# Moving a block's transfers from GpSimd's queue to SyncE's in a LayerNorm, attention and ternary feed-forward kernel

## The chip, the core and the metric

The kernel runs on one core of a Trainium2 chip. A core has a matrix engine (TensorE, PE in the profile; its weight loads are PEld), a vector engine (VectorE, DVE), an activation engine (ScalarE, ACT), a general engine (GpSimd, POOL) and a sequencer without arithmetic (SyncE, SP). Each engine works through its own list of instructions in order; a DMA is an instruction on one of these lists, and while it waits for its turn or for a semaphore, everything behind it on that list waits too. The metric is the device time of one execution in microseconds.

## The reference

The input x is 2048 rows of 256 numbers, all float32. With xn the layer norm of x, the output is x plus an attention of 16 heads of 128 over xn, plus a gated feed-forward over xn whose weights are rounded to -1, 0 or 1:

```
qkv = einsum('bsd,ed->bse', xn, Wqkv)          # 3 x 16 heads of 128
logits = einsum('bqhd,bkhd->bhqk', q, k) * 128 ** -0.5
out = einsum('bhqk,bkhd->bqhd', softmax(logits), v)
y = x + einsum('bse,de->bsd', out, Wout) + ffn(xn)
ffn(xn) = (sigmoid(xn @ t(w1)) * (xn @ t(w2))) @ t(w3)
```

Here t(w) divides a weight by its mean magnitude, rounds, clips to -1..1 and transposes.

## The kernel before, in words

After a lead-in (norm, first head's q, k and v, the feed-forward), the kernel walks 64 *blocks*: a block is one head and 512 of the 2048 queries, four blocks to a head. A block has four *steps* of 128 queries (t = 0 to 3), and one pass of the main loop (line 965) is one step. The pass does work for two places at once: scores, exponentials and exchange for step v, and, six steps behind (`LEAD`), the product with the values for block n, step t (`divmod(u, TB)`).

In a pass `scores` puts 128 by 2048 logits in PSUM (PE), DVE takes their maxima, ACT takes exponentials into `p`. The product with v needs the exponentials transposed. `exchanged` (line 595) moves the off-diagonal quarters of `p` into `part` with twelve DMAs, ten issued from SP and two from ACT, and ACT copies the four diagonal quarters; `transposed` (line 652) lets DVE turn 32 by 32 pieces of `part` into `R`, two passes later. `part` has two buffers, so the exchange of step v waits until DVE has transposed step v - 2. GpSimd forms differences of `R` (line 677) for a fast product with seven instead of eight multiplications, `weighted` (line 706) is that product, and `copied` and `added` combine its quarters in `oU`.

The order on every engine is written out by hand (`manual_schedule`): an instruction stands on its engine's list where the loop calls it.

Around a block there are transfers that are no exchange:
- `inverses` (line 615) stores the reciprocals of the softmax sums to DRAM (`rd`), and `spread` (line 630) reads them back to all partitions into `oT`, by which `added` scales `oU`.
- `put_away` (line 777) stores `oU` to DRAM (`od`).
- The output projection is also a fast product. It is done two heads (a *group*) at a time, in blocks 0 to 3 of the next group: `o_fetched` (line 787) brings two heads' stored outputs back into the three slots of `o3`, `o_product` (line 803) multiplies them with the group's part of Wout, into the PSUM tile `pow`, and `o_read` (line 817) lets DVE add the result to the running sum of the output, `osums`. `osums` holds two of the four query quarters; `y_moved` (line 793) stores one to DRAM (`yd`) and brings the next one back. `o_moved` (line 826) and `between` (line 929) say in which block and step each of these is called.
- `load_weights` (line 73) loads the weights of the next group.

Most of them are called from `between`, at the end of a pass and so after that pass's exchange. The times at which the sum's data must be there follow from the two-step rhythm: of the fetches and returns in `o_moved`, `y_moved` at (block, step) (0, 0), (1, 3) and (2, 0) is read by `o_read` in the next pass, and `o_fetched` at (1, 0) and (3, 0) is read by `o_product` at the end of the next pass. The DMAs of the last blocks (lines 858, 867, 913 and 957) stand outside the change.

Of the kernel before, what the change touches and what calls it, by code (L numbers as in the profile page):

```python
# [20 lines left out]
def layernorm_attention_bitffn_kernel(  # L21
# [14 lines left out]
    nc = tc.nc  # L36
# [9 lines left out]
    TB = QB // P  # L46
# [4 lines left out]
    G = 2  # L51
# [21 lines left out]
    def load_weights(g: int, what: str, queue=nc.sync):  # L73

        if what == "o":
            w = wpool.tile([P, G, DM], F32, tag="wvo", name=f"wo{g}")
            src = woutT[g * G * D : (g + 1) * G * D, :].rearrange("(h p) e -> p h e", p=P)
        else:
            tag = "wvo" if what == "v" else f"w{what}"
            w = wpool.tile([P, KC, G * D], F32, tag=tag, name=f"w{what}{g}")  # L80
            lo = "qkv".index(what) * HD + g * G * D
            src = wqkvT[:, lo : lo + G * D].rearrange("(c p) e -> p c e", p=P)
        queue.dma_start(w, src)
        weights[g, what] = w
# [60 lines left out]
    def weight_sums(h: int):  # L145
        wk, wq = (weights[h // G, i][:, :, bass.ts(h % G, D)] for i in "kq")
        w = wpool.tile([P, 4, D], F32, tag="ws", name=f"ws{h}")
        add, sub = ALU.add, ALU.subtract
        nc.gpsimd.tensor_tensor(w[:, 0], wq[:, 0], wq[:, 1], add)
        nc.gpsimd.tensor_tensor(w[:, 1], w[:, 0], wk[:, 0], sub)  # L150
        nc.gpsimd.tensor_tensor(w[:, 2], wk[:, 0], wq[:, 0], sub)
        nc.gpsimd.tensor_tensor(w[:, 3], wk[:, 1], w[:, 1], sub)
        ws[h] = w
# [70 lines left out]
    o3 = const.tile([P, 3, QB], F32, tag="o3", name="o3")  # L224
# [57 lines left out]
    def v_read(g: int, m: int, second: bool, pm):  # L282
# [14 lines left out]
    ods = [  # L297
        [away.tile([P, G, QB], F32, tag=f"od{g}_{c}", name=f"od{g}_{c}") for c in range(NB)]
        for g in range(2)
    ]  # L300
    rds = [away.tile([P, 32], F32, tag=f"rd{i}", name=f"rd{i}") for i in range(2)]
# [313 lines left out]
    def inverses(n: int):  # L615
        if n >= NBK - NB:

            r = small.tile([P, TB], F32, tag="rlast", name=f"rlast{n}")
            nc.vector.tensor_tensor(r, sums[n][:, :, 0], sums[n][:, :, 1], ALU.add)
            nc.vector.reciprocal(r, r)  # L620
            rbs[n] = r
            return
        ri, riT = rinvs[n % 2]
        nc.vector.tensor_reduce(ri[:, :TB], sums[n], AX.X, ALU.add)
        nc.vector.reciprocal(ri[:, :TB], ri[:, :TB])

        nc.vector.transpose(riT, ri)  # L627
        nc.gpsimd.dma_start(rds[n % 2], riT)  # L628

    def spread(n: int):  # L630

        if n < NBK - NB:
            r = rds[n % 2].rearrange("(j c) r -> j (c r)", c=32)[:, : TB * 32]
            nc.gpsimd.dma_start(
                oT.rearrange("p (j x) -> p j x", j=P // 32), r.partition_broadcast(P)
            )
            rbs[n] = oT
# [3 lines left out]
    for n in range(1, len(blocks)):  # L641
        a, b, c, d, e = roles[-1]
# [142 lines left out]


    def o_fetched(g: int, b: int, head: int, slot: int):
        nc.gpsimd.dma_start(o3[:, slot], ods[g % 2][b][:, head])

    def o_difference(slot: int, x: int, y: int):  # L790
        nc.gpsimd.tensor_tensor(o3[:, slot], o3[:, x], o3[:, y], ALU.subtract)

    def y_moved(b: int, back: bool):
        y, yd = osums[:, 1 - b % 2], yds[b]
        nc.gpsimd.dma_start(*((yd, y) if back else (y, yd)))

    def o_sums(g: int):
        w = weights[g, "o"]
        sums_of(w[:, :, :P], w[:, :, P:], f"wos{g}")
# [26 lines left out]
    def o_moved(g: int, i: int, t: int):  # L826

        pair, a = divmod(i, 2)
        b, more = 2 * pair, pair == 0
        keep = g == H // G - 2 and pair  # L830
        if (a, t) == (0, 0):
            y_moved(b + 1, False)
        elif (a, t) == (0, 1):
            o_fetched(g, b, 1, 1)
        elif (a, t) == (0, 3):
            o_difference(2, 1, 2)
        elif (a, t) == (1, 0):
            o_fetched(g, b + 1, 1, 0)
        elif (a, t) == (1, 1):
            if not keep:  # L840
                y_moved(b, True)
            if more:
                o_fetched(g, b + 3, 1, 2)
        elif (a, t) == (1, 2):
            if more:
                o_fetched(g, b + 3, 0, 1)
                o_fetched(g, b + 2, 0, 0)
        elif (a, t) == (1, 3) and more:
            y_moved(b + 2, False)
            o_difference(1, 1, 0)  # L850
            o_difference(2, 2, 1)
# [4 lines left out]
    def fetched_back(b: int):  # L856

        nc.gpsimd.dma_start(xnT[:, :, bass.ts(b, QB)], yds[b])

    def x_fetched(b: int):  # L860
        if b % 2 == 0:
            tag, bufs = (("v", 3), ("kT", 2))[b // 2]
            y = kvpool.tile([P, S], F32, tag=tag, name=f"ya{b}", bufs=bufs)
            y = y.rearrange("p (b t d) -> p b t d", b=2, d=DM)
            sofar[b], sofar[b + 1] = y[:, 0], y[:, 1]
        nc.gpsimd.dma_start(
            sofar[b], x[b * QB : (b + 1) * QB, :].rearrange("(t p) d -> p t d", p=P)
        )
# [60 lines left out]
    def between(n: int, t: int):  # L929

        g, i = divmod(n, GB)
        last = NBK - NB

        if t == 1:
            if i == GB - 1 and n < last:
                load_weights(g, "o", nc.gpsimd)
        if t == 2:
            if i == NB - 1 and g + 1 < H // G:
                load_weights(g + 1, "v", nc.gpsimd)
            elif n == last - 1:  # L940
                load_weights(g, "o", nc.gpsimd)
        if g and i < NB:
            o_moved(g - 1, i, t)
        elif n < last:
            if i == GB - 2:
                if t < 3:
                    o_fetched(g, *((0, 0, 0), (1, 0, 1), (1, 1, 2))[t])
                else:
                    o_difference(1, 1, 0)
                    o_difference(2, 2, 1)  # L950
            elif (i, t) == (GB - 1, 2):
                y_moved(0, False)
        if n < last and (i, t) == (GB - 1, 3):
            o_sums(g)
        if n >= last - 1 and t == 2:
            b = n + 1 - last
            nc.gpsimd.dma_start(o3[:, b % 2], ods[(H - 2) // G % 2][b][:, 0])
        if (n, t) in ((last - 2, 3), (last - 1, 0)):
            fetched_back(n + 2 - last)
        if t == 0 and n in (last - 3, last - 2, last, last + 1):  # L960
            x_fetched((last - 3, last - 2, last, last + 1).index(n))

    behind = []
    with tc.manual_schedule():
        for u in range(-LEAD, (NBK - 1) * TB):
            n, t = divmod(u, TB)
            v = u + LEAD
            lead_in = u < 0
            more = v < NBK * TB
            h, b = blocks[v // TB] if more else (H, 0)  # L970
# [7 lines left out]
            g, i = divmod(n, GB)  # L978
# [22 lines left out]
            if t == 0 and n >= 0:  # L1001
                if 0 < n <= NBK - NB:
                    put_away(n - 1)
                differences(n, "T1b")
            elif t == 1 and n >= 0:
                differences(n, "T2h")
                if n >= NB and n % GB < NB and n % 2 == 0 and n < NBK - NB:
                    o_difference(0, 2, 0)
                differences(n, "T3b")
                spread(n)  # L1010
                if blocks[n][1] == 0:
                    v_combined(blocks[n][0], 2)
                    v_combined(blocks[n][0], 3)
                differences(n, "T4")
            elif t == 3 and -1 <= n < NBK - 2:
                differences(n + 1, "T1a")
                if n % 2 and n % GB < NB <= n < NBK - NB - 2:
                    y_moved(n % GB, True)
                differences(n + 1, "T3a")
                if n >= 0 and blocks[n + 1][1] == 0:  # L1020
                    v_combined(blocks[n + 1][0], 0)
                    v_combined(blocks[n + 1][0], 1)
# [23 lines left out]
                    q_piece(1, b)  # L1046
            if b == NB - 1 and h + 2 < H:
                if h % G == 0 and v % TB in (0, 1):
                    load_weights(h // G + 1, "qk"[v % TB], nc.gpsimd)
                if v % TB == 3:  # L1050
                    weight_sums(h + 2)
            twice = seven and twice
            if t == 2 and -1 <= n < NBK - 1:
                inverses(n + 1)
# [30 lines left out]
            if u >= 0:  # L1085
                if t == 0:
                    differences(n, "T2l")
                between(n, t)

        n = NBK - 1  # L1090
# [50 lines left out]
```

## Time and profile before

| | |
|---|---|
| median of 3 runs | 2158.83 us (2158.8 to 2162.86) |
| profiled execution, its own time | 2159.7 us |
| its span | 2157.9 us |
| PE busy | 2143.5 us |
| DVE, ACT, POOL busy | 1756.1, 1375.1, 1579.3 us |
| bytes moved by DMA | 304.34 MB, 141 GB/s in the mean |
| DMAs issued from SP in the main loop | 2560 exchanges, 64 KB each |

The profile gives, for one execution, the busy time of each engine, the DMAs with the median time from issue to landing, and groups of instructions by line. A wait is written as engine and line, what ended the wait, then the total in us, how often, and the longest. A row of the timeline has its start and its duration in us from the span's start, then engine, line, operation and tiles; "SPq" is SP's queue of DMAs, and what stands in square brackets is the idle time of the engine before the row and what ended it.

### The profile page before, as it was taken

What the parts mean: (1) busy time and instruction counts of PE and PEld (TensorE: products, weight loads), DVE (VectorE), ACT (ScalarE), POOL (GpSimd) and SP (SyncE); (2) the same over time, 40 slices, a digit from 0 to 9 for tenths busy, and PEclk for the clock granted to TensorE, in tenths of its full rate; (3) what the DMA queues carried; (4) which work ended last, traced back from release to release, by engine and by line L of the source; (5) the groups of instructions that cost most, each with busy time, mean ns of one, the idle gap of its engine ahead of it and who ended that gap; (6) DMA issues with size and microseconds to landing.
All of it is one profiled execution on the core that took longest, in us unless ns stands there. A gap on an engine that the chain in (4) does not pass through costs nothing. (4 is left out here: it accounts for less than half of the span.)

```text
span 2157.9 us, 41390 instructions
## 1 busy us (share of the span) xinstructions
PE 2143.5 (99%) x14018; PEld 1207.6 (56%) x14018; DVE 1756.1 (81%) x2394; ACT 1375.1 (64%) x2414; POOL 1579.3 (73%) x1010
## 2 busy tenths in 40 slices
PE   9999999999999999999999999999999999999999
PEld 6745445445655555555555455655555555555556
DVE  6577887888888887888788888788888888788885
ACT  5587766666666666666666666666666666666773
POOL 0067767987678867887768876788767887788873
PEclk9999999999999999999999999999999999999999
DMA  2055555575556655566555754556555665556663
GB/s 94 39 119 139 132 117 136 148 187 142 121 140 160 166 141 128 136 184 157 123 128 142 189 151 110 140 145 180 149 122 135 157 173 143 127 138 184 174 151 95
DMA packets 182341, 304.34 MB, mean 141 GB/s; under 512 B 55088, under 2 KB 60592, under 8 KB 182128
## 3 DMA queue, kind: packets, MB, share of 16 engines
q1 hardware_dynamic: 127856, 175.21, 31.9%
q0 software_dynamic: 28720, 91.97, 17.5%
q10 hardware_dynamic: 25552, 34.51, 6.2%
q8 instruction: 111, 1.82, 0.4%
q14 instruction: 102, 0.84, 0.1%
HBM read 65.60 MB, written 34.54 MB: 46 GB/s over the span
## 5 line engine op out<-in xcount | busy, mean ns | idle before, releaser
L677 POOL TENSOR_TENSOR R<-R 128x1024 f32<-128x1024 f32 x441 | 1175.5, 2673 | 144.4 <-DVE R L657 84.7
L94 PE MATMUL s<-kT,qT 128*64 128x512 f32 x4000 | 907.4, 592 | 1.0 <-ACT p L589 0.8
L613 ACT COPY part<-p 32x512 f32<-32x512 f32 x1024 | 630.7, 616 | 417.7 <-issue 306.5
L579 DVE TENSOR_REDUCE mx<-s 128x1 f32<-128x1024 f32 x512 | 618.2, 1220 | 230.5 <-PE s L94 216.7
L589 ACT ACTIVATE p<-s,nm 128x1024 f32<-128x1024 f32 x512 | 565.9, 1110 | 207.8 <-PE pw L94 101.6
L657 DVE STREAM_TRANSPOSE R<-part 128x1024 f32<-128x1024 f32 x512 | 605.1, 1220 | 34.1 <-DMA part<-p 24.4
L94 PEld LDWEIGHTS s<-kT,qT 128*64 128x64 f32 x4000 | 331.7, 137 | 476.2 <-issue 431.8
L724 PE MATMUL av<-R,v 128*64 128x256 f32 x3728 | 531.2, 379 | 1.5 <-DVE oU L750 1.3
L724 PE MATMUL av<-R,st 128*64 128x256 f32 x3024 | 457.7, 379 | 2.5 <-ACT oU L742 1.3
L724 PEld LDWEIGHTS av<-R,v 128*64 128x64 f32 x3728 | 357.7, 137 | 109.7 <-issue 43.9
L724 PEld LDWEIGHTS av<-R,st 128*64 128x64 f32 x3024 | 305.5, 137 | 143.0 <-issue 50.6
L628 POOL DMA_DIRECT2D rd<-r x60 | 33.4, 556 | 154.2 <-DVE r L627 153.9
L742 ACT COPY oU<-av 64x256 f32<-64x256 f32 x248 | 90.7, 366 | 84.5 <-PE av L724 77.0
L780 POOL DMA_DIRECT2D od<-oU x60 | 34.0, 567 | 125.0 <-DVE oU L754 125.0
L750 DVE TENSOR_TENSOR oU<-av,oU 64x256 f32<-64x256 f32 x248 | 101.8, 411 | 27.4 <-ACT oU L742 24.7
L94 PE MATMUL pvw<-wv,xnT 128*64 128x256 f32 x896 | 107.6, 379 | 0.0
L94 PEld LDWEIGHTS pvw<-wv,xnT 128*64 128x64 f32 x896 | 74.8, 137 | 45.7 <-issue 24.2
L589 ACT ACTIVATION_READ_ACCUMULATOR p<-s,nm 128x1 f32 x512 | 100.3, 196 | 0.0
L824 DVE TENSOR_TENSOR osums<-pow,osums 128x512 f32<-128x512 f32 x108 | 72.5, 682 | 29.3 <-DMA osums<-yd 18.3
L94 PE MATMUL pw<-t,ws 128*64 128x512 f32 x336 | 88.4, 592 | 0.0
L160 POOL TENSOR_TENSOR t<-xnT 128x512 f32<-128x512 f32 x4 | 5.1, 1271 | 107.1 <-DMA part<-p 107.1
L200 DVE TENSOR_TENSOR kT<-pw,kT 128x512 f32<-128x512 f32 x112 | 76.8, 686 | 1.8
(153 smaller groups left out, 1484.4 us busy)
## 6 DMA issues: line engine op xcount, KB each, us to landing
part<-p SPq DMA_DIRECT2D x2560, 64.0 KB, 2.3
part<-p ACTq DMA_DIRECT2D x512, 64.0 KB, 2.6
o<-od POOLq DMA_DIRECT2D x74, 256.0 KB, 3.9
oT<-rd POOLq DMA_DIRECT2D x60, 256.0 KB, 5.5
od<-oU POOLq DMA_DIRECT2D x60, 256.0 KB, 2.7
osums<-yd POOLq DMA_DIRECT2D x28, 512.0 KB, 4.8
yd<-osums POOLq DMA_DIRECT2D x26, 512.0 KB, 3.5
yd<-yT SPq DMA_DIRECT2D x4, 512.0 KB, 2.6
```

Of the source, the lines that this page charges most:

```text
L94: nc.tensor.matmul(out[c * HP : (c + 1) * HP], lhs[:, c * HP : (c + 1) * HP], rhs, start=start, stop=stop, skip_group_check=True,)
L200: nc.vector.tensor_tensor(k, pk, base, ALU.add)
L579: nc.vector.tensor_reduce(mx[:, i : i + 1], s, AX.X, ALU.max)
L589: nc.scalar.activation(p, s, AF.Exp, bias=nm, scale=SCALE, accum_out=sums[n][:, t, i : i + 1],)
L613: nc.scalar.copy(*ends(j, j))
L657: nc.vector.transpose(to[:, t % 2, 2 * i : 2 * i + 2], part.rearrange("p g (s c) -> p g s c", s=2),)
L677: nc.gpsimd.tensor_tensor(o, x, y, ALU.subtract)
L724: nc.tensor.matmul(av[i * HP : (i + 1) * HP, half], l[:, kk], moving(s, kk), start=start, stop=(k == units[r] - 1), skip_group_check=True,)
L742: nc.scalar.copy(u[op, oq], av[ap, half])
L750: nc.vector.tensor_tensor(u[p, q], av[p, half], u[p, q], ALU.add)
L780: nc.gpsimd.dma_start(ods[h // G % 2][b][:, h % G], oU)
L824: nc.vector.tensor_tensor(to, pm, y, ALU.add)
```

## The change

All of a block's transfers but the store of its sums (`put_away`) issue from SP's queue: the reciprocals' store and their return, the fetches of heads' outputs, both directions of the running sum, and the weights of the next group. Their places in the program stay as they were; only the list on which they stand is another.

```
     def inverses(n: int):
-        nc.gpsimd.dma_start(rds[n % 2], riT)
+        nc.sync.dma_start(rds[n % 2], riT)
     def spread(n: int):
-            nc.gpsimd.dma_start(
+            nc.sync.dma_start(
                 oT.rearrange("p (j x) -> p j x", j=P // 32), r.partition_broadcast(P)
             )
     def o_fetched(g: int, b: int, head: int, slot: int):
-        nc.gpsimd.dma_start(o3[:, slot], ods[g % 2][b][:, head])
+        nc.sync.dma_start(o3[:, slot], ods[g % 2][b][:, head])
     def y_moved(b: int, back: bool):
         y, yd = osums[:, 1 - b % 2], yds[b]
-        nc.gpsimd.dma_start(*((yd, y) if back else (y, yd)))
+        nc.sync.dma_start(*((yd, y) if back else (y, yd)))
...
-                load_weights(g, "o", nc.gpsimd)
+                load_weights(g, "o")
-                load_weights(g + 1, "v", nc.gpsimd)
+                load_weights(g + 1, "v")
-                load_weights(g, "o", nc.gpsimd)
+                load_weights(g, "o")
...
-                    load_weights(h // G + 1, "qk"[v % TB], nc.gpsimd)
+                    load_weights(h // G + 1, "qk"[v % TB])
```

`load_weights` without a queue uses SP's (its default, line 73).

## The prediction

> **What bounds the kernel now.** I read the page's busy shares first, then the waits of PE, DVE and SP, then the timeline around one of the head-group sums. The page says that PE works the whole time: 2157.9 us of span less 2143.5 us busy leaves 14.4 us in which PE is idle, and the granted clock is full in all forty slices. So nothing that shortens another engine can gain more than those 14.4 us, and whatever makes PE wait is paid in full.
>
> ```profile
> PE 2143.5 (99%) x14018; PEld 1207.6 (56%) x14018; DVE 1756.1 (81%) x2394; ACT 1375.1 (64%) x2414; POOL 1579.3 (73%) x1010
> part<-p SPq DMA_DIRECT2D x2560, 64.0 KB, 2.3
> o<-od POOLq DMA_DIRECT2D x74, 256.0 KB, 3.9
> osums<-yd POOLq DMA_DIRECT2D x28, 512.0 KB, 4.8
> yd<-osums POOLq DMA_DIRECT2D x26, 512.0 KB, 3.5
> yd<-yT SPq DMA_DIRECT2D x4, 512.0 KB, 2.6
> ```
>
> The waits show where it is already tight. DVE waits 17 times for the running sum to come back from DRAM (`osums<-yd`), and three times PE's product `pow` waits for DVE in turn. SP's own waits, nearly all for DVE to free a `part` buffer, are the only room its queue has.
>
> ```profile
> DVE osums L824 <- DMA osums<-yd: 18.3, 17, 2.0
> PE pow L94 <- DVE osums L824: 1.7, 3, 0.6
> SPq L611 <- DVE R L657: 206.1, 169, 3.2
> SPq L611 <- DMA part<-p: 93.5, 107, 2.6
> ```
>
> Now the timeline around the second of seven such sums (start and duration in us). Each SPq line is the ten exchanges of one step; each POOL line is a load of the sum's data; each L824 line is DVE adding to that sum; each `pow` line is PE's product that needs a head's fetched sums.
>
> ```profile
> 648.68 7.38 SPq L611 DMA_DIRECT2D part<-p  x10
> 680.41 7.11 SPq L611 DMA_DIRECT2D part<-p  x10
> 705.64 8.37 SPq L611 DMA_DIRECT2D part<-p  x10
> 714.20 7.84 SPq L611 DMA_DIRECT2D part<-p  x10
> 744.61 6.83 SPq L611 DMA_DIRECT2D part<-p  x10
> ...
> 650.69 0.55 POOL L795 DMA_DIRECT2D osums<-yd  x1
> 705.42 0.55 POOL L795 DMA_DIRECT2D osums<-yd  x1
> 714.32 0.55 POOL L795 DMA_DIRECT2D osums<-yd  x1
> ...
> 655.55 1.29 DVE L824 TENSOR_TENSOR osums<-pow,osums 128x512 f32<-128x512 f32 x2 [0.76 <-DMA osums<-yd]
> 712.29 0.69 DVE L824 TENSOR_TENSOR osums<-pow,osums 128x512 f32<-128x512 f32 x1 [1.77 <-DMA osums<-yd]
> 719.07 1.28 DVE L824 TENSOR_TENSOR osums<-pow,osums 128x512 f32<-128x512 f32 x2
> ...
> 689.22 1.06 PE L94 MATMUL pow<-o,wos 128*64 128x512 f32 x4
> 753.58 1.06 PE L94 MATMUL pow<-o,wos 128*64 128x512 f32 x4
> ```
>
> The reader should see that the loads start at about the same moment as SP begins a step's ten exchanges, that the ten take 7 to 8 us, and that the consumer comes 5 to 7 us after the load's issue. In program order the load stands behind those ten exchanges; on POOL's queue that costs it nothing, on SP's queue it must wait for all of them.
>
> **The change part by part.** It removes 273 DMA issues from POOL (60 rd, 60 oT, 70 of the 74 o<-od, 54 between osums and yd, 29 weights) and adds them to SP; in the built program the orders of PE, DVE and ACT are untouched, and 74 DMAs stay on POOL.
>
> *Loads that a step needs within the next one.* Five per group of two heads, in seven groups: the sum's return at blocks 0, 1 and 2 of the group's walk, and the fetch of a head's output at blocks 1 and 3. On SP the earliest landing is the end of the ten exchanges, plus 0.05 us to the next instruction, plus the landing time of the DMA section (4.8 us for osums<-yd, 3.9 us for o<-od). Against the consumer's start in the rows above:
> - 648.68 + 7.38 = 656.06, landing 660.9, DVE wants it at 655.55: 5.4 us late
> - 680.41 + 7.11 = 687.52, landing 691.5, PE wants it at 689.22: 2.3 us late
> - 705.64 + 8.37 = 714.01, landing 718.9, DVE wants it at 712.29: 6.6 us late
> - 714.20 + 7.84 = 722.04, landing 726.9, DVE wants it at 719.07: 7.8 us late
> - 744.61 + 6.83 = 751.44, landing 755.4, PE wants it at 753.58: 1.8 us late
>
> The same subtraction in all seven groups gives means of 4.9, 2.5, 7.0, 7.3 and 2.7 us, 24.4 a group and 171 us in all. A loss moves queue and consumer alike, so the terms add. For PE's own two waits nothing covers. For DVE's three, everything behind L824 on DVE waits: the next transposes of R, so POOL's differences and PE's av, and the PSUM bank of the next pow product. The cover is what PE tolerates: DVE's 1.77 us wait at 712.29 is followed by a PE gap of 0.48 us at 713.13, so about 1.3 us; the waits of before already use 0.97, 1.07 and 0.59 us of it (means). That leaves 1.3 us a group, 9 us in all: 171 - 9 = 162 us.
>
> *How fast SP's transfers land.* No load of this kind is issued from SP in the steady part. The nearest row is the 512 KB store: 2.6 us from SP, 3.5 us from POOL, 0.9 us less. Those four SP stores ran in the lead-in with no exchanges about, so part of the difference is the idle DMA engines. By 0.9 us on 35 loads the sum falls 31 us, by nothing it stays; I take half, 16 us: 162 - 16 = 146 us. For the low end a load lands as the faster rows do (2.6 us for 512 KB, and 2.4 us for 256 KB, a little over the exchanges' 2.3): 2.2 x 21 + 1.5 x 14 = 67 us off 162, so 95 us. For the high end it lands as the slowest of before, 6.9 and 5.5 us: 2.1 x 21 + 1.6 x 14 = 67 us more, 229 us.
>
> [...]
>
> *The other moved DMAs.* rd (60), oT (60), stores of the sum (26), weights (29) and the other 56 fetches and 7 early returns are needed two steps or more after their issue; what covers them is that distance. Of the fetches, the last at block 1 comes nearest to being late: it stands behind the exchanges that end at 705.32 us, lands at about 709.9 with one fetch ahead of it, and is wanted at block 2's first product at 708.13, but that pass already loses 6.6 us to the sum's return, which contains it. The early return is the closest: SP ends its exchanges at 641.01 us and DVE reads at 646.78, while 4.8 us are needed. Each costs SP an issue, 0.68 us by the ten in 6.83: 273 x 0.68 = 186 us, against about 280 us in which SP waits for buffers, copies and exps, so the queue still keeps up on average. Around block 1 of a group some eight stand in two steps, 5.4 us against about 2.5 us of room; the 2.9 us too many are about what PE has by then lost at the first fetch, so I add nothing. The exchanges behind them slip by as much, but the transposes that need them start at a median of 5.0 us after the last landing. If that cover fails, SP's 93.5 us of waits for earlier exchanges could double: 0 to +94, I take 0. A wait newly placed on SP, for the r of the reciprocals, ends before the `part` buffers come free that the following exchanges need anyway: 0.
>
> *Lead-in.* Through most of the first five blocks the transposes start 0.1 to 0.3 us after their last exchange lands, so there is no slack. Four or five moved DMAs there give about 3 us; ends 0 and 7 us, the longest wait that POOL had for the first wq.
>
> *POOL set free.* 170 us of issues leave POOL, 73% busy. PE's 14.4 us of idle hold about 6 us of start and tail, so this gives 0 to 8 us; the same loads that come late keep it from showing, so 0.
>
> Sum: 146 + 3 = +149 us on the profiled execution's 2159.7 us, 2309 us. The median of the runs, 2158.83 us, is 0.9 us below that execution, less than the sum can tell.
>
> **The rivals.**
> 1. *SP's queue overflows* (chance 0.14): the late loads and, besides, exchanges that land after the transposes want them. For it: exchange steps of 8 us around the sums. Against: the 5.0 us median slack. Price: 162 + 94 = 256 us, some 2415 us.
> 2. *The late loads are mostly hidden* (0.10): DVE slides and catches up in its idle time, and SP's loads land fast. It decides if PE tolerates some 5 us instead of 1.3; then the three DVE terms of 4.9, 7.0 and 7.3 leave 4.3 us and PE's two 5.2 less a shorter landing, 3 to 5: some 8 us a group, 56 us, 2215 us. Against it: PE's gap after only 1.77 us.
> 3. *POOL's freedom wins, faster* (0.03): POOL's 170 us were what PE's last gaps came from, and SP reaches each load before POOL did. Price -8 us, 2152 us. It decides only where SP's ten exchanges end before POOL's issue time; at the loads above SP is 5 to 8 us later.
> 4. *No difference* (0.03): every load lands in time, 2160 us. That the change does not do what it says is excluded by the built order.
>
> **How the numbers follow.** The forecast's case has 0.70; its own range is 95 to 229 us plus lead-in, 2255 to 2395 us. Rivals 2 and 1 lie at 2215 and 2415. For 8 in 10 I take 2245 to 2395. No change that a measurement of this kernel can tell is 0.2%, 4.3 us. Faster 0.03, same 0.03, slower 0.94.
>
> **What the profile after would show.** DVE's wait for osums<-yd grows from 18.3 us to 100 us or more; PE gets waits before `pow` for DVE and for o<-od that total 100 us or more; PE's busy time barely moves while its idle rises from 14 to 150 us; the loads' issue stands right behind ten exchanges on SP. Wrong would be: PE's idle spread over all blocks, with transposes waiting for `part` (rival 1), or DVE waits of 5 us with no PE gap behind them (rival 2).

## The result and the profile after

The changed kernel takes 2346.28 us (median of 5 runs, 2339.33 to 2347.96) against 2161.01 us before: a ratio of 1.085, 95% interval 1.083 to 1.087. The profiled execution took 2339.33 us and has a span of 2337.5 us, 179.6 us more than before. The forecast was 2309 us, range 2245 to 2395.

The page's first rows and its DMA issues, to be held against those of before:

```profile
PE 2196.4 (94%) x14018; PEld 1202.4 (51%) x14018; DVE 1753.4 (75%) x2394; ACT 1375.0 (59%) x2414; POOL 1412.2 (60%) x737
...
part<-p SPq DMA_DIRECT2D x2560, 64.0 KB, 2.0
part<-p ACTq DMA_DIRECT2D x512, 64.0 KB, 2.2
o<-od SPq DMA_DIRECT2D x70, 256.0 KB, 3.3
oT<-rd SPq DMA_DIRECT2D x60, 256.0 KB, 5.2
od<-oU POOLq DMA_DIRECT2D x60, 256.0 KB, 2.9
osums<-yd SPq DMA_DIRECT2D x28, 512.0 KB, 3.7
yd<-osums SPq DMA_DIRECT2D x26, 512.0 KB, 3.9
```

PE does the same 14018 matmuls, yet it is busy 2196.4 us instead of 2143.5, and idle 2337.5 - 2196.4 = 141.1 us instead of 14.4. So the 179.6 us have two parts: 126.7 us of waiting, which was forecast, and 52.9 us in which the same matmuls took longer, which was not. Of the moved transfers the loads of the sum and of the outputs land sooner from SP, 3.7 us after the issue instead of 4.8 and 3.3 instead of 3.9; the stores of the sum land later, 3.9 instead of 3.5.

The waits of DVE and PE, in total, how often and the longest:

```profile
DVE osums L824 <- DMA osums<-yd: 131.2, 20, 10.5
PE pow L94 <- DMA o<-od: 60.4, 21, 7.3
PE pow L94 <- DVE osums L824: 20.9, 5, 6.5
PE pvw L94 <- DMA wv<-in_wqkvT_dram: 7.7, 4, 5.8
```

DVE's wait for the returned sum rose from 18.3 to 131.2 us. PE's wait for the fetched outputs did not exist before. The last row was not foreseen at all: PE waits for v weights.

The timeline around the second head-group sum, the same place as in the prediction:

```profile
745.92 0.38 SPq L83 DMA_DIRECT2D wk<-in_wqkvT_dram  x1
746.41 8.96 SPq L611 DMA_DIRECT2D part<-p  x10
755.41 0.58 SPq L795 DMA_DIRECT2D osums<-yd  x1
760.90 6.41 SPq L611 DMA_DIRECT2D part<-p  x10
767.36 0.58 SPq L795 DMA_DIRECT2D osums<-yd  x1
...
759.00 0.69 DVE L824 TENSOR_TENSOR osums<-pow,osums 128x512 f32<-128x512 f32 x1 [8.99 <-DMA osums<-yd]
771.12 1.29 DVE L824 TENSOR_TENSOR osums<-pow,osums 128x512 f32<-128x512 f32 x2 [3.11 <-DMA osums<-yd]
...
759.84 1.98 PE L94 MATMUL pow<-o,wos 128*64 128x512 f32 x4 [6.94 <-POOL o L791]
```

Each return of the sum is issued right behind ten exchanges (746.41 + 8.96 = 755.37), as argued, and DVE stands 8.99 us until it lands. PE's next product adds to the tile that DVE has just read, and it starts at 759.84 us, 0.15 us after DVE is done (759.00 + 0.69), with a wait of 6.94 us. The view puts this wait down to a difference on POOL that happens to end in the same moment; at the same place of the seven groups it names DVE's read five times. The four matmuls of that product take 1.98 us, where the row of before has 1.06.

Windows of the same execution show why (start and end, length, busy us of each engine with its count of instructions, then PE's granted clock, the DMA share and GB/s):

```profile
740.00:752.00 12.00, 11.46 (x76) 5.83 (x74) 9.47 (x12) 9.48 (x16) 7.35 (x6) 1.00 0.70 199
752.00:760.00 8.00, 1.06 (x11) 0.55 (x9) 1.00 (x2) 0.77 (x3) 7.92 (x5) 0.84 0.50 148
760.00:764.00 4.00, 4.00 (x10) 1.19 (x11) 2.87 (x4) 0.73 (x2) 4.00 (x2) 0.50 0.30 71
764.00:772.00 8.00, 8.00 (x56) 4.21 (x54) 3.54 (x5) 4.77 (x9) 4.24 (x5) 0.99 0.54 156
```

After the 8 us in which PE hardly works, its granted clock is 0.50 for the next 4 us, and then full again. Over the whole span the mean granted clock is 0.979, 1.000 before. The trace's record of the clock has 22 stretches at 0.50, 99.0 us in all, and PE is busy for 79.9 us of them. At half the clock (four matmuls of the product take 1.98 us there) that is an estimated 40 us of lost work, so the slower clock accounts for 40 of the 52.9 us; the other 13 stay open.

### The profile page after: what moved, and what is told of

Its sections match the earlier page's. It is cut to its first block, busy times and chain, and to the rows that moved or that the text cites. A ratio compares the mean times of both kernels' runs of the same rounds, so it can differ in the third digit from the quotient of the medians.

```text
span 2337.5 us, 41238 instructions
## 1 busy us (share of the span) xinstructions
PE 2196.4 (94%) x14018; PEld 1202.4 (51%) x14018; DVE 1753.4 (75%) x2394; ACT 1375.0 (59%) x2414; POOL 1412.2 (60%) x737
## 4 chain that ended last, share of the span: by engine, by line
PE 60%; SPq 13%; DMA 12%; DVE 10%; issue 3%; ACT 1%; POOL 1%; DVEq 0%; ACTq 0%; POOLq 0%
PE s L94 23%; PE av L724 20%; SPq L611 12%; DVE R L657 5%; DMA part<-p 5%; PE pw L94 4%; PE pvw L94 4%; DMA osums<-yd 2%; DVE mx L579 2%; DMA o<-od 2%; PE ph L457 2%; PE pow L94 2%; PE pf L480 1%; DVE oU L750 1%; PE s L576 1%
## 5 line engine op out<-in xcount | busy, mean ns | idle before, releaser
L94 PE MATMUL s<-kT,qT 128*64 128x512 f32 x4000 | 924.0, 602 | 2.4 <-ACT p L589 2.4
L824 DVE TENSOR_TENSOR osums<-pow,osums 128x512 f32<-128x512 f32 x108 | 72.4, 681 | 194.9 <-DMA osums<-yd 131.2
L94 PE MATMUL pow<-o,wos 128*64 128x512 f32 x224 | 71.3, 712 | 77.6 <-DMA o<-od 45.5
L791 POOL TENSOR_TENSOR o<-o 128x512 f32<-128x512 f32 x56 | 71.9, 1285 | 66.4 <-DMA o<-od 65.9
```

What stands on the lines that cost most here:

```text
L94: nc.tensor.matmul(out[c * HP : (c + 1) * HP], lhs[:, c * HP : (c + 1) * HP], rhs, start=start, stop=stop, skip_group_check=True,)
L824: nc.vector.tensor_tensor(to, pm, y, ALU.add)
```

## The experiments

Two questions were open: do the five urgent loads a group account for the loss, and what is PE's slower clock worth? A place is written (block of the group's walk, step). "Idle" is the span less PE's busy time of one profiled execution, and all ratios are against runs of the kernel before on the same chip.

| run | median us | ratio (95%) | PE idle | PE busy | mean clock |
|---|---|---|---|---|---|
| before | 2161.01 | 1 | 14.4 | 2143.5 | 1.000 |
| after | 2346.28 | 1.083 to 1.087 | 141.1 | 2196.4 | 0.979 |
| five_moved | 2324.62 | 1.074 to 1.077 | 121.3 | 2205.8 | 0.970 |
| y_moved | 2238.39 | 1.035 to 1.038 | 67.1 | 2168.2 | 0.990 |
| o_moved | 2246.24 | 1.039 to 1.041 | 71.0 | 2173.7 | 0.985 |
| o_moved_filled | 2225.14 | 1.029 to 1.032 | 42.6 | 2175.6 | 0.997 |
| rest_moved | 2250.63 | 1.040 to 1.043 | 84.7 | 2163.6 | 0.985 |
| rest_but_rd | 2224.39 | 1.029 to 1.032 | 57.2 | 2164.3 | 0.988 |
| six_kinds_kept | 2236.18 | 1.035 to 1.038 | 67.1 | 2166.1 | 0.989 |
| urgent_kept | 2199.83 | 1.018 to 1.021 | 39.3 | 2157.3 | 0.998 |
| five_first | 2283.71 | 1.056 to 1.059 | 99.9 | 2181.9 | 0.978 |
| five_middle | 2272.24 | 1.050 to 1.053 | 90.9 | 2178.6 | 0.983 |
| all_first | 2280.57 | 1.054 to 1.062 | 102.8 | 2172.6 | 0.983 |
| only_five_first | 2161.87 | 1.000 to 1.002 | 14.6 | 2142.2 | 1.000 |

The rows of five_moved and o_moved_filled are from the slowest and the fastest of their four executions; the other three have clocks of 0.975 or 0.976 and 0.995 or 0.996.

To see where a run loses, the start of each pass's L582 instruction (the negated maxima) is set against the kernel before; the table has how much further it falls behind, in us, as the mean of seven groups, at the pass where a loss becomes visible. A loss at one place shows in the next pass or the one after.

| run | (0,2) | (1,2) | (2,1) | (2,2) | (3,2) | (4,1) | first four blocks, once |
|---|---|---|---|---|---|---|---|
| after | 4.4 | 4.0 | 9.4 | 2.4 | 5.4 | 1.1 | 9.6 |
| five_moved | 3.1 | 6.7 | 6.6 | 2.2 | 7.3 | 0 | 0.6 |
| rest_moved | 0 | 0 | 9.2 | 0 | 0 | 2.3 | 7.8 |
| five_first | 0 | 0 | 8.7 | 0 | 0 | 7.7 | 8.0 |
| five_middle | 1.2 | 0 | 8.6 | 1.3 | 1.2 | 4.3 | 8.9 |

In the passes (0,3) and (2,3) about 1 us is won back where (0,2) and (2,2) lose. The last column is mostly a loss at the place (4,1) of the first group, which the seven do not include.

**Only the five urgent loads moved.** To the kernel before:

```
-            y_moved(b + 1, False)
+            y_moved(b + 1, False, nc.sync)
...
-            o_fetched(g, b + 1, 1, 0)
+            o_fetched(g, b + 1, 1, 0, nc.sync)
...
-            y_moved(b + 2, False)
+            y_moved(b + 2, False, nc.sync)
```

`o_fetched` and `y_moved` take a queue here, as in all the runs; without one they keep that of the kernel that the run starts from.

> The kernel before with only the five urgent loads of each group, 35 in all, moved to SP. Place theory: by the rows of before and the landings measured after (3.7 and 3.3 us), lateness 20 us a group less 1.3 us of cover gives 131 us of PE idle, and the half-speed clock after the stalls adds some 40 us: 2320 to 2335 us. Load theory: 35/273 of 185 us, about 2185 us.

2324.62 us, inside the range expected: 35 loads of 273 by themselves cost 164 us, where the whole change costs 185. So the number of issues is not their cause. That it is their place, and not SP as such, is shown by only_five_first below. The split was not as expected, 107 us more idle instead of 131, and 62 us more busy time instead of 40.

**All but the five moved.** The changed kernel with these three calls given `nc.gpsimd`.

> The changed kernel with the five urgent loads of each group (the sum's returns at block and step (0,0), (1,3), (2,0) and the fetches at (1,0), (3,0)) left on POOL: 238 of the 273 transfers move. Place theory (the five stand behind ten exchanges on SP): nearly all of the loss goes, 2161 us and some 5 to 10 us for the late weights and the lead-in, about 2168 us, half-speed clock near the 2.4 us of before. Load theory (SP's queue has too many issues): 238/273 of the 185 us stays, about 2320 us.

2250.63 us, 90 us over before: the theory that the place of the five explains the loss had this at 2168 and is refuted as a full account. And 164 + 90 is not 185, so the parts do not add. By the second table the two runs lose 24.2 and 11.6 us a group over all passes, their sum is 35.8, and the changed kernel loses 24.1. More than half of the difference, 6.4 us a group, is at (2,1), where both runs lose: there the late return and the late fetches hold up PE in the same pass, and one wait hides a part of the other. Of rest_moved's own loss most is at (2,1), 9.2 us a group or 64 us. SP's queue and PE there:

```profile
714.89 0.58 SPq L795 DMA_DIRECT2D yd<-osums  x1
715.64 0.33 SPq L788 DMA_DIRECT2D o<-od  x1
716.01 0.80 SPq L83 DMA_DIRECT2D wq<-in_wqkvT_dram  x1
719.69 0.32 SPq L628 DMA_DIRECT2D rd<-r  x1
720.12 7.34 SPq L611 DMA_DIRECT2D part<-p  x10
727.57 1.02 SPq L788 DMA_DIRECT2D o<-od  x2
...
732.16 1.97 PE L94 MATMUL pow<-o,wo 128*64 128x512 f32 x4 [7.73 <-DMA o<-od]
```

This is the pair of fetches at (1,2), which the prediction had put at 1.8 us late (709.9 against 708.13) and set aside. Here it is PE's whole wait, 7.73 us. Ahead of the ten exchanges (7.34 us) stand four more transfers, and between 716.81 and 719.69 us the queue stands at `rd<-r`. The run below was made on the reading that it waits there for DVE, but DVE had done r long before:

```profile
SPq L628 <- DMA part<-p: 2.8, 1, 2.8
...
712.82 0.21 DVE L627 STREAM_TRANSPOSE r<-r 128x32 f32<-128x32 f32 x1
```

The first line is SP's wait between 700 and 732 us: it ends with the landing of an exchange, at 719.62 us.

**The same without rd on SP.** Line 628 back to POOL.

> As with the five urgent loads of each group on POOL, and the reciprocals' store on POOL too. On SP that store waited 2.9 us for DVE in the pass before the fetches at block 1, step 2, and held the ten exchanges behind it. If that wait is a part of their lateness, PE's waits of 7 us shrink to about 4 us and the clock falls less often: 24 us and some 10 us less than 2250.6 us, about 2216 us. If the exchanges alone make the fetches late, it stays near 2245 us.

2224.39 us, 26 us less than with it (34 expected), or 23 us when each is held against the kernel before on its own chip. Sixty 16 KB stores off SP's queue are worth that much, and PE's waits for the fetches at (1,2) fall from 50.0 to 31.1 us. But the reason expected, a store that holds the queue because its data is late, is not what the traces show. In rest_moved five of the seven stores at this place issue 0.1 us after the instruction ahead of them, and the other two, with 2.9 and 2.3 us, wait for the landing of an exchange, with r ready 6 us before they issue. What does change over the whole run is that SP's waits for its own earlier transfers fall from 159.5 to 130.5 us and its waits for DVE to free a buffer grow from 60.7 to 109.1: the queue is earlier. How 60 short issues do that stays open.

**The two fetches at (1,2) on POOL as well.** To rest_moved, so with rd on SP again.

> As with the five urgent loads of each group on POOL, and the two fetches at block 1, step 2 on POOL too: 224 of the 273 transfers move. If those fetches are a sixth urgent kind, and the only reason for PE's waits of 7 us at block 2's first product, then the 9.2 us a group lost there go, 64 us of 90; what stays are the late v weights (2.3 us a group), the last Wout weights and the lead-in, about 26 us: 2187 us. If SP's many issues are the reason, little changes: 2235 us or more.

2236.18 us: by the number the second case, 2235 or more, yet not by its reason. The 9.2 us at (2,1) are gone, but 7.2 us a group appear at (4,1), where rest_moved had 2.3. It is the v weights, loaded at (3,2) and needed two passes later; PE's largest wait in this run:

```profile
PE pvw L94 <- DMA wv<-in_wqkvT_dram: 33.5, 7, 5.8
```

Before, such a load landed at 765.79 us, and PE's first weight load from it started at 772.07, 6.3 us later; behind ten exchanges, which take 6 to 9 us, little or nothing of that is left. The likely reading of the second table is that where PE loses time earlier in the group, SP catches up and the weights are nearly in time, and where it does not, they are late: a second, smaller reason why the parts don't add.

**The v and output weights on POOL too.** Of the loads that PE waits for in the views above, none is then on SP.

> Beyond that, the weights of v and of the output projection stay on POOL: 209 of the 273 transfers move (reciprocals, their return, the sum's stores, q and k weights, the fetches that nothing waits for). If the urgent loads account for all of the loss: 2161 us, at best 2153 us as POOL has some 115 us less to issue. If SP's many issues cost something by themselves: 2180 us or more.

2199.83 us, 1.9% over before, so the 209 transfers that were thought not to be in a hurry cost 42 us. The loss is spread, 0.6 to 2.0 us at five passes of a group. The largest, 2.0 us at (0,1), is one more late load, the early return of the sum, issued at (7,2) and read two passes later:

```profile
640.48 6.21 SPq L611 DMA_DIRECT2D part<-p  x10
646.73 0.59 SPq L795 DMA_DIRECT2D osums<-yd  x1
...
651.13 0.69 DVE L824 TENSOR_TENSOR osums<-pow,osums 128x512 f32<-128x512 f32 x1 [2.26 <-DMA osums<-yd]
```

In the seven groups DVE waits 1.4 to 4.3 us for it, 17.9 in all; before there was no such wait. For the rest of the loss the views of DVE's and SP's waits show what it is, in this run and then before:

```profile
DVE R L657 <- DMA part<-p: 74.2, 62, 4.7
SPq L611 <- DMA part<-p: 204.1, 137, 5.9
SPq L611 <- DVE R L657: 4.7, 12, 0.5
```

```profile
DVE R L657 <- DMA part<-p: 24.4, 17, 3.8
SPq L611 <- DMA part<-p: 93.5, 107, 2.6
SPq L611 <- DVE R L657: 206.1, 169, 3.2
```

Before, SP waited 206 us for DVE to free a buffer: the queue was early. With the 209 transfers it waits 4.7 us for that, its waits for its own earlier transfers double to 204 us, and DVE waits for exchanges 62 times. From the last landing of an exchange to its transpose the median is 1.4 us, where it was 5.0. SP's queue has hardly any slack left.

**The urgent loads ahead of the exchanges.** All 273 on SP, but the five come first in their pass, or after five of the ten exchanges:

```
     def exchanged(v: int, at: int = 0, then=None):
...
+            if m == at and then:
+                then()
             queue = nc.sync if m < SP_DMAS else nc.scalar
...
-                exchanged(v)
+                exchanged(v, 0, lambda: o_soon(n, t))
```

`o_soon` makes the three calls of the urgent loads, and `o_moved` no longer does; in the second run the 0 is a 5.

> The changed kernel with the five urgent loads still on SP, but issued ahead of the pass's ten exchanges. Place theory: they are issued some 7 us sooner and land before they are wanted; about 2168 us, as with the five on POOL. If SP's transfers as such are the trouble (its ring carries exchanges and loads in one file), or the number of issues, it stays above 2300 us.

> The changed kernel with the five urgent loads on SP after five of the ten exchanges. Place theory: 3.4 us earlier than in the changed kernel, so lateness of 0.4, 2.5 and 2.8 us at the three returns and none at the fetches: 31 us of idle at most, 0 to 15 us by the clock and 7 us for the rest, 2190 to 2225 us. Load theory: as the changed kernel, about 2340 us.

2283.71 and 2272.24 us, both far above what was expected. The second table separates the causes: the losses at (0,2), (1,2), (2,2) and (3,2) are zero in the first run and 1.3 us or less in the second, as expected if the place behind the exchanges is what makes the five late. What stays is what rest_moved has too, the fetches at (1,2) and the v weights, and the latter now cost 7.7 and 4.3 us. That the middle is faster than the front was not foreseen; the table puts the difference at the v weights.

**More transfers ahead.** As in five_first, with the fetches at (1,2) and the v and output weights ahead of their pass's exchanges as well. The early return at (7,2) stays behind its own.

> All 273 transfers on SP as in the changed kernel, but every urgent one (the five, the fetches at block 1, step 2, the v and output weights) issued ahead of its pass's ten exchanges. If only the place behind its own pass's exchanges matters: 2161 to 2170 us. If SP is also behind by a pass around block 1, because of the number of its issues, the sum's return at (1,3) still comes 6 to 8 us late, behind a store and a weight load and the exchanges of the pass before: some 60 us with the clock, and 8 us of lead-in, about 2229 us.

2280.57 us: above even the 2229 of the second case. PE's wait for weights is gone, and 10.8 us a group stand at (2,1), 4.2 at (0,1). The second is the early return again, for which DVE waits 3.2 to 6.6 us in each group. SP's queue at the first:

```profile
720.04 8.35 SPq L613 DMA_DIRECT2D part<-p  x10
728.44 0.58 SPq L797 DMA_DIRECT2D yd<-osums  x1
729.12 0.39 SPq L83 DMA_DIRECT2D wk<-in_wqkvT_dram  x1
729.56 0.82 SPq L797 DMA_DIRECT2D osums<-yd  x1
730.48 7.40 SPq L613 DMA_DIRECT2D part<-p  x10
```

The return of (1,3), at 729.56 us, is ahead of its own pass's exchanges and still stands behind those of the pass before, because SP is a pass behind here. With all 273 on SP, no place in the pass that was tried saves the kernel; one with the early return ahead too was not tried.

**The five ahead, the others on POOL.** The kernel before with the five on SP by the same `o_soon`.

> The kernel before with only the five urgent loads moved to SP, ahead of the pass's ten exchanges; all others stay on POOL. Place theory: the loads land before they are wanted, DVE's 18.3 us of waits for the returned sum go and with them PE's few gaps there: 2152 to 2161 us. If SP's transfers as such are the trouble: above 2300 us.

2161.87 us against 2158.47, ratio 1.0012 (1.0003 to 1.0021). The five can go through SP at no cost worth speaking of: the losses of 164 us come from 35 loads standing behind ten exchanges, not from SP or its kind of transfer. Nor is there a gain: DVE's wait for the sum falls from 18.3 to 6.4 us, and PE's idle stays at 14.6 us. No version beat the kernel before.

**The two kinds of the five by themselves.** The sum's returns, and the fetches.

> The kernel before with only the three urgent returns of the running sum moved to SP, 21 loads. Place theory: lateness with the 3.7 us landing, less the cover, 14.6 us a group, 102 us of idle, and some 30 us by the clock: about 2290 us. If DVE could catch up (its cover 5 us instead of 1.3), about 2200 us.

> The kernel before with only the two urgent fetches moved to SP, 14 loads, which PE itself waits for. Place theory: about 2.0 us of idle each, 28 us, and 10 to 20 us by the clock: about 2204 us. Without an effect of the clock 2189 us.

2238.39 us: the 21 returns cost 53 us of idle, half of the 102 expected, and 25 us of busy time. The loads are as late as expected, for DVE waits 15.4 us a group for them:

```profile
DVE osums L824 <- DMA osums<-yd: 107.7, 21, 6.8
```

But PE loses only half of that, so DVE catches up far more than the 1.3 us that one small gap in the trace of before had suggested. And 2246.24 us: the 14 fetches cost 57 us of idle instead of 28, and 30 us of busy time. Their landing is why:

```profile
o<-od POOLq DMA_DIRECT2D x60, 256.0 KB, 3.9
...
o<-od SPq DMA_DIRECT2D x14, 256.0 KB, 5.7
```

From SP these 14 fetches land in 5.7 us here, and in 3.0 us (median) in the changed kernel. What they meet here is POOL's `oT<-rd`, in flight for 3.1 to 5.6 us of each; at 700 to 707 us the DMA engines are 98% busy. In the changed kernel that load stands behind the fetch on SP's list. In five_moved 13 of the 14 meet it and take 4.7 to 5.4 us, and the one that does not takes 3.3. No run changes that alone.

**Filling PE's wait.** The fetches on SP, and PE does two products that nothing uses, into the tile that the next product overwrites:

```
+        if m % NB == 3 and second:
+            for _ in range(2):
+                in_halves(opms[g], w[:, 1, :P], o3[:, 1], True, True)
         in_halves(opms[g], lhs, o3[:, slot], start, True)
```

> As with the two urgent fetches on SP, and PE does two useless products (1.7 us by 0.43 us a half and pass) into the same PSUM tile just before each of the 14 waits, 24 us of work more that the next product overwrites. If idle PE loses its clock: the stall's idle is filled, no half-speed stretches at these places, and the time falls by 5 to 15 us although work is added, to about 2190 us. If the clock has nothing to do with the idle: not faster than without the filler, 2204 us or more.

2225.14 us, 21 us faster than o_moved (5 to 15 expected), with some 24 us more work. PE's busy time is 2175.6 us against 2173.7: the added work is paid for by the clock, whose mean goes from 0.985 to 0.997. The stretches at 0.50 fall from 68.3 us to 13.7. The group of the awaited product, without and with the filler:

```profile
L94 PE MATMUL pow<-o,wos 128*64 128x512 f32 x224 | 68.5, 685 | 58.9 <-DMA o<-od 57.1 <-DVE osums L824 1.7
```

```profile
L94 PE MATMUL pow<-o,wos 128*64 128x512 f32 x224 | 60.7, 620 | 31.6 <-DMA o<-od 31.2 <-DVE osums L827 0.4
```

The mean matmul goes from 685 to 620 ns, before it is 594 ns.

## Why the prediction was right, and where it was not

The sign, the mechanism and the size held: the returns and fetches that a step needs within the next one stand behind ten exchanges, and five_moved shows that they alone cost 164 us, and only_five_first shows that it is the place. Within the sum, terms were wrong in both directions.

- *The term missing.* A wait of PE was counted as its own length. It can also be followed by a granted clock of 0.50, in the changed kernel for 3.4 to 10.2 us at a time: that is 40 of the 52.9 us of longer busy time, which the forecast put at nothing ("PE's busy time barely moves"). The prediction read the full clock in the slices of before as settled. No wait of PE in that trace is longer than 1.5 us, so it does not show what a longer one does.
- *The returns, 4.9, 7.0 and 7.3 us with 1.3 us of cover.* Too much: y_moved has 53 us of idle, 7.5 a group, for 17.9 after the cover; 3.3 of the difference is the landing, 1.1 us shorter each. The rest is DVE, which catches up more than 1.3 us. In the changed kernel, too, PE waits only 5.9 us a group behind the returns. The one gap behind a wait of 1.77 us was too little to read a cover from. The 0.9 us by which the returns were to land sooner on SP came near for them (1.1), but the row it was read from did not hold: the stores of the sum land later from SP, 3.9 against 3.5 us.
- *The fetches, 2.5 and 2.7 us.* Near in the changed kernel, where PE waits 2.9 and 3.6 us for them, though partly by luck, for they also land sooner than the 3.9 us assumed. The landing on SP depends on what else moves: 5.7 us in o_moved, 3.0 in the changed kernel.
- *The other moved DMAs, 0.* Wrong: rest_moved costs 90 us by itself. The fetch at (1,2) was seen and set aside as contained in another loss; the v weights were said to have two steps or more, and have 6.3 us, no more than ten exchanges take; the early return was called the closest, and DVE waits for it in urgent_kept. The wait for r was put at 0: the stores of r cost 23 us in rest_but_rd's comparison, but SP does not wait for r at the place of the loss, so this step stays open. In the changed kernel these losses fall largely into the others: after less five_moved is 22 us.
- *Rival 1, the overflowing queue.* It was given 0.14, with SP's waits for its own transfers doubling. That is what urgent_kept shows, 93.5 to 204.1 us. In the changed kernel they are 102.1 us only, most likely because PE's stalls give the queue time. The mean arithmetic (186 us of issues against 280 us of room) said that the queue keeps up; it keeps up only without the slack that the exchanges lived on.
- *Lead-in, 3 us.* 9.6 us; 5.8 of it is PE's wait for the first v weights of the loop, which is the late load of (4,1) and not the late exchanges that the term was for.
- *POOL set free, 0.* Held: no run with fewer issues on POOL was faster than before.

So 2309 was near 2346 partly by chance: PE's idle came to 127 us against 149 forecast, with the returns priced far too high and other late loads in their place, and the longer busy time made up for the rest and more.

## What to carry to other kernels

Before a DMA is moved to another queue, write down for each one when its data must be there, and what stands ahead of it on the new list at that moment; the landing time is the smaller term (here 3.0 to 5.7 us for the urgent loads, with ten exchanges of 6 to 9 us ahead of them). A queue whose engine is "idle, waiting for buffers" is early, and that earliness is slack which added issues spend: here 209 of them turned 206 us of such waiting into 4.7. When PE is the bound, price a stall at its length plus the slower clock behind it: here an estimated 40 us beside 126.7 us of waiting.

## What was not expected of the hardware

- PE's granted clock fell to 0.50 after some gaps and not after others, and the length of the gap alone does not decide it. In the changed kernel the gap of 2.45 us before 805.18 us was followed by half speed, the longer one of 2.70 us before 1038.51 us was not:

```profile
805.20:808.40 3.20, 3.20 (x8) 1.06 (x10) 0.69 (x1) 1.36 (x3) 0.00 (x0) 0.50 0.46 110
```

```profile
1038.60:1042.00 3.40, 3.40 (x17) 1.34 (x19) 3.40 (x5) 0.07 (x1) 3.40 (x3) 1.00 0.19 45
```

- Useless matmuls in PE's waits made o_moved 21 us faster.
- The same 256 KB fetch from SP took 5.7 us to land behind ten exchanges with `oT<-rd` on POOL's queue, 3.0 us with it behind the fetch on SP's, and 3.1 us ahead of the exchanges (only_five_first). The 512 KB return took 3.6 to 3.7 us from SP behind the exchanges (y_moved, the changed kernel) and 4.6 ahead of them (only_five_first), 4.8 from POOL before.
